# Loading down_w a second time and rounding it later, in a gated quantised MLP on one core

## The chip, the core and the metric

The kernel runs on one core of one Trainium2 chip. The metric is the device time in microseconds of one execution. A core has a matrix engine (PE, or TensorE), three engines for elementwise work (DVE or VectorE, ACT or ScalarE, POOL or GpSimd), a sequencer that issues nearly all DMAs of this kernel (SP or SyncE) and 16 DMA engines that carry them out. Each engine runs its own instructions in program order and waits on semaphores.

## The reference

x is 4 batches of 1024 tokens by 512. The weights are norm_w (512 by 128), up_w (4096 by 512) and down_w (512 by 2048).

```python
scale = cond @ norm_w.T + 1.0
ms = jnp.mean(x * x, axis=-1, keepdims=True)
h = x * (scale[:, None, :] * jax.lax.rsqrt(ms + EPS))
u = h @ up_w.T
val, gate = jnp.split(u, 2, axis=-1)
h = val * jax.nn.gelu(gate, approximate=False)
hq = act_quant(h)            # per token: round to -128..127 steps of max|h| / 127
wq = weight_quant(down_w)    # 1 / mean|down_w| as scale, round to -1, 0, 1
return hq @ wq.T + x
```

What matters here is weight_quant. It needs the mean of |down_w| over the whole matrix before the first element can be rounded, and its result, one of three values per element, is needed only by the second product.

## The kernel before

**Batches and slots.** The four batches are worked on one after the other, each in 16 slots (j is 0 to 15 within a batch, g is 16 b + j over all). One slot multiplies 128 rows of the gate half and 128 rows of the value half of up_w with the batch's 1024 tokens. Operands are split into a high and a low 16-bit part, so that a product is several matmuls added up in PSUM. The first batch uses the plain form: `plain_half(j, h)` is 12 matmuls of 512 columns for the gate (PSUM tile pg, line 601), a Gelu of it on ACT (line 629), 12 matmuls for the value (pv, line 601) and one DVE instruction that multiplies the two into H (line 633). h is 0 or 1, the half of the tokens. The later batches use a scheme with seven products of six matmuls in a slot (`slot`, products on line 586): PSUM tiles A, B and E, three ACT copies between them (lines 668, 675, 680) and two Gelus (lines 685, 701). In the first slot of the second batch (g = 16) two of the seven products belong to no slot before it and are missing.

**PSUM.** The tag "A" has two buffers, "B" one and "E" two. In the first batch pg of the first half lies in B, pg of the second half in A, and both pv in E. So the pv of one half waits until the DVE instruction of line 633 two halves earlier has read its bank, and line 633 waits for the Gelu of line 629.

**While the first batch runs**, the other engines prepare what the later batches need: they scale and split the rows of up_w and spill them to DRAM (s_dram; lines 355 and 400 on SP), and they normalise and split the tokens of the second batch in four groups of 256 (class `Tokens`, keys 6, 8, 10 and 12 in `TOKENS`: a group is normalised and summed in slot j and split by `high` and `low` and turned by a transposing DMA, `turn`, line 572, in slot j + 1). The tiles of a group are tagged xn (or am), xt and nx; each tag has one buffer. `turn` writes them into R[:, 1].

**down_w.** Eight parts of 128 by 1024 floats (512 KB each) are loaded into R[:, 1] at the start (`d_load`, line 444) and summed by absolute value (`d_sum`) up to slot 3; the mean is known in slot 4. `d_round(n)` multiplies part n by the scale and adds a large constant on ACT (line 464), `d_put(n)` takes the sign of the rounded part on ACT (line 473) and writes fp8 into a tile tn, two parts to one tile. After every second part a transposing DMA writes tn into wd (line 475). R[:, 1] is also where the turned tokens of the second batch go, so that the parts must be rounded before `turn` overwrites them: `D_ROUND` gives the slots. wd is read for the first time by the sums of weights in slots 9 and 10 of the second batch (`D_SUM_AT`).

**Fillers.** From the second batch on, two lists (`Filler`) hold DVE and ACT work; `run("x")`, `run("y")` and `run("z")` in a slot take items from their front as long as a budget lasts (on ACT 2.7 us at x and 1.1 us at y of an ordinary slot).

**SP order.** SP issues in program order, and it waits on behalf of a DMA before it issues it; what comes behind has to wait too. In slots 13 and 15 of the first batch, and in every slot of the second, it issues the loads of the weights for a slot that lies two ahead: `s_load_x(g)` brings the parts 5 and 6 (line 418, plain) and 0 to 2 (line 416, transposed), `s_load_y(g)` the rest. They go into SXY[:, (g + 1) % 2] and wait until the slot that used that buffer has been multiplied. The first product of a slot reads part 5, the second part 0, the fourth in time of g = 16 part 6.

A tile is handed on only when the last reader of its former content is done, also where that reader comes later in the program than the instruction that takes the buffer over.

Of the kernel before, what the change touches and what calls it, by code (L numbers as in the profile page):

```python
# [9 lines left out]
F32 = mybir.dt.float32  # L10
F16 = mybir.dt.float16
BF16 = mybir.dt.bfloat16
F8 = mybir.dt.float8e4
I32 = mybir.dt.int32
AF = mybir.ActivationFunctionType
# [4 lines left out]
P = 128  # L20
EXPONENT = 0x7F800000
MAGIC = 1.5 * 2.0**23
# [29 lines left out]
def glu_quant_kernel(  # L52
# [10 lines left out]
    PE, ACT, DVE, POOL, SP = nc.tensor, nc.scalar, nc.vector, nc.gpsimd, nc.sync  # L63
# [14 lines left out]
    wpool = ctx.enter_context(tc.tile_pool(name="work", bufs=2))  # L78
# [9 lines left out]
    unmagic = cpool.tile([P, 1], F32, name="unmagic")  # L88
# [24 lines left out]
    for n in range(0, P, 32):  # L113
        c = slice(n, n + 32)
# [118 lines left out]
    def cond_spread(dg, b0, b1, tag):  # L233
        n = b1 - b0
        pd = bank(tag, {"po": 3}.get(tag, 2), [P, B], f"pd_{b0}")[:, :n]
        PE.matmul(pd, ones[:n, :], dg, start=True, stop=True)
        return pd
# [42 lines left out]
    def w_load(j, ts=(1, 0)):  # L280
        if j > 2:
            SP.dma_start(out=wn(j), in_=up_v[j])
            return
        for t in ts:
            SP.dma_start(out=wn(j)[:, t], in_=up_v[j][:, t])
# [27 lines left out]
    def w_range(j, t0=0, t1=2):  # L313
        w_factor(j, w_largest(j, t0, t1), t0, t1)

    def w_gain(j):
        DVE.tensor_tensor(sg0[:, j, :], sw[:, j, :], dx[:, 0:1].to_broadcast([P, 2]), ALU.mult)
# [6 lines left out]
    def w_scale(j, ts=(1, 0), eng=None):  # L324
        eng = eng or (ACT if j >= ROWS else POOL)
        for t in ts:
            w, r = wn(j)[:, t], iv[j][:, t : t + 1]
            if eng is ACT:
                ACT.activation(w, w, AF.Copy, scale=r)
            else:  # L330
                eng.tensor_scalar(w, w, r, 1.0, ALU.mult, ALU.mult)
# [16 lines left out]
    def w_rows(j):  # L348

        v = H[:, ROW_SLOT.get(j, 15 + j % 2)].bitcast(F16).rearrange("p t d -> p (t d)")  # L350
        n = v.rearrange("p (n w f) -> p n w f", n=4, w=2)
        f = wn(j).rearrange("p t (n f) -> p (t n) f", n=2)
        ACT.copy(n[:, :, 0], f)
        DVE.tensor_tensor(n[:, :, 1], f, n[:, :, 0], ALU.subtract)
        SP.dma_start_transpose(
            s_tile(j)[:, 3:7].rearrange("p n w (k f) -> p (n w k) f", k=2), v
        )
# [19 lines left out]
    def s_sums(j):  # L377
        v = wn(j).rearrange("p t (n f) -> p t n f", n=2)
        a11, a12, a21, a22 = v[:, 1, 0], v[:, 1, 1], v[:, 0, 0], v[:, 0, 1]
        POOL.tensor_tensor(sf[:, 0], a21, a22, ALU.add)  # L380
        POOL.tensor_tensor(sf[:, 2], a11, a21, ALU.subtract)
        POOL.tensor_tensor(sf[:, 1], sf[:, 0], a11, ALU.subtract)
        POOL.tensor_tensor(sf[:, 3], a12, sf[:, 1], ALU.subtract)
# [6 lines left out]
    def s_high(j):  # L390
        for s, f in s_parts(j):
            ACT.copy(s[:, :, 0], f)
# [37 lines left out]
    wsc = cpool.tile([P, 1], F32, name="wsc")  # L430
    wsum = cpool.tile([P, 2 * NK], F32, name="wsum")
    HF = FF // 2
    ND = 2 * NK

    def d_part(n):
        return R[:, 1, n * HF : (n + 1) * HF]

    def d_at(n):

        return n // 4 + 2 * (n % 2), n // 2 % 2, n % 2  # L440
# [5 lines left out]
    def d_sum(n):  # L446
        jk = wpool.tile([P, HF], BF16, name=f"djk_{n}", tag="gm", bufs=1)
        ACT.activation(jk, d_part(n), AF.Abs, accum_out=wsum[:, n : n + 1])

    def d_total():  # L450
        part = sm.tile([P, 1], F32, name="wpart", bufs=1)
        DVE.tensor_reduce(part, wsum, AX.X, ALU.add)
        return part

    def d_mean(part):
# [2 lines left out]
        DVE.tensor_scalar(wmean, pm, 1.0 / (D * FF), 1e-5, ALU.mult, ALU.max)  # L458
        DVE.reciprocal(wsc, wmean)

    def d_round(n):

        dn = d_part(n)
        ACT.activation(dn, dn, AF.Copy, scale=wsc, bias=MAGIC)

    tn = []

    def d_put(n):
        _, u, y = d_at(n)
        if y == 0:  # L470
            tn.append(wpool.tile([P, HF], BF16, name=f"tn_{n}", tag="v"))
        t8 = tn[-1].bitcast(F8).rearrange("p (f y) -> p f y", y=2)
        ACT.activation(t8[:, :, y], d_part(n), AF.Sign, bias=unmagic, saturate=False)
        if y:
            SP.dma_start_transpose(wd[:, n // 4, u], tn[-1])

# [131 lines left out]
    def gains(b):  # L608
        sg[b] = sm.tile([P, NJ, 2], F32, name=f"sg_{b}", tag="sg")
        DVE.tensor_scalar(sg[b], sw, dx[:, b : b + 1], None, ALU.mult)  # L610
# [12 lines left out]
    def plain_half(j, h, between=nothing):  # L623
        whole = j == WHOLE
        tag = ("po", 3) if whole else ("A", 2) if h or j == 1 else ("B", 1)
        pg = bank(*tag, name=f"pg_{j}_{h}")
        plain(j, 1, h, pg)
        t1 = wpool.tile([P, TOK], F32, name=f"g_{j}_{h}", tag="t1")
        ACT.activation(t1, pg, AF.Gelu, scale=gain(j, 1))
        between()  # L630
        pv = bank(*(("po", 3) if whole and not h else ("E", 2)), name=f"pv_{j}_{h}")
        plain(j, 0, h, pv)
        DVE.scalar_tensor_tensor(h_half(j, h), pv, gain(j, 0), t1, ALU.mult, ALU.mult)
# [80 lines left out]
    def pair_max(b, i, h):  # L714

        v = h_slots(b * NJ + 2 * i, 2)[:, :, h].rearrange("p j t -> p t j")
        m = m_view(b, h)
        if i == 0:
            return [lambda: DVE.tensor_reduce(m, v, AX.X, ALU.max, apply_absolute_value=True)]
        gm = []  # L720

        def largest():
            gm.append(wpool.tile([P, TOK], F32, name=f"gm_{b}_{i}_{h}", tag="gm", bufs=1))
            DVE.tensor_reduce(gm[0], v, AX.X, ALU.max, apply_absolute_value=True)  # L724

        return [largest, lambda: DVE.tensor_tensor(m, m, gm[0], ALU.max)]  # L726
# [343 lines left out]


    D_SUM = {0: (4, 5), 1: (6, 7), 2: (2, 3), 3: (0, 1)}
    D_ROUND = {5: (0, 1), 6: (2,), 7: (3,), 9: (4,), 10: (5,), 11: (6,), 12: (7,)}
    D_MEAN = 4
    TOKENS = {6: 0, 8: 1, 10: 2, 12: 3}
    LARGEST = {
# [5 lines left out]
    def next_tokens(j):  # L1082

        if j in TOKENS:
            toks[j] = toks[j + 1] = Tokens(1, TOKENS[j])
            toks[j].load()

    def s_all(j):
        s_high(j)
        s_low(j, POOL)  # L1090
        s_spill(j)

    def first_batch(j, sc):

        if j + 2 <= LATE:
            w_load(j + 4)
        if j >= 4:
            next_tokens(j + 2)
        t = toks.get(j)
        odd = t is not None and j not in TOKENS  # L1100
        n = j + 2
        rows = LATE <= n < NJ
        if j + 1 < LATE:
            s_sums(j + 1)
        elif rows:
            s_sums(n)
        if j + 3 < NJ:
            w_range(j + 3)
            w_gain(j + 3)
        if j == D_MEAN:  # L1110
            part = d_total()
        plain_half(j, 0)
        for i, h in LARGEST.get(j, ()):
            for f in pair_max(0, i, h):
                f()
        if n < LATE:
            w_scale(n)
            w_rows(n)
        if j + 1 < LATE:
            s_all(j + 1)  # L1120
        if t and not odd:
            t.norm()
        for m in D_ROUND.get(j, ()):
            d_round(m)
            d_put(m)
        if t and not odd:
            t.scale(sc)
            t.sums()
        if j + 2 > LATE and j + 5 < NJ:
            w_load(j + 5)  # L1130
        if odd:
            t.high()
            t.low(DVE)
        if odd:
            t.turn()
        plain_half(j, 1)
        if j == 3:
            pd = cond_spread(dg, 1, B, "po")
            cond_undo(pd, 1, B)
            cond_rows()  # L1140
        if j == D_MEAN:
            d_mean(part)
        own = rows and j + 1 >= LATE

        def next_rows():
            if LATE <= j + 3 < NJ:
                w_scale(j + 3)
                w_rows(j + 3)

        if odd:  # L1150
            next_rows()
        if own:
            s_high(n)
            s_low(n, POOL)
        if not odd:
            next_rows()
        if own:
            s_spill(n)
        elif rows:
            s_sums(n)  # L1160
            s_all(n)
            w_load(j + 5)
        for n in D_SUM.get(j, ()):
            d_sum(n)
        if j in (NJ - 3, NJ - 1):
            s_load_x(NJ + (j - NJ + 3) // 2)
            s_load_y(NJ + (j - NJ + 3) // 2)
# [165 lines left out]
    state = {}  # L1333
    for b in range(1, B):
        dve, act = Filler(), Filler()
        gains(b)
        am = am_tile(b - 1)
        dq = state[b - 1] = sm.tile([P, 2 * NA], F32, name=f"dq_{b}", tag="dq")
# [120 lines left out]
    b = B - 1  # L1459
# [109 lines left out]
    for h in range(2):  # L1569
# [21 lines left out]
        for a in range(NA):  # L1591
            c, xr = slice(0, HALF * ys[a]), XR[:, h * NA + a]
            down_mm(b, h, a, pos[a][:, c], range(cut, NJ), 0, ys[a])
            down_end(b, h, a, pos[a][:, c], xr[:, c], dq, c)
    c = slice(HALF, D)
# [29 lines left out]
```

## Time and profile before

| what | value |
|---|---|
| median of 3 runs | 725.08 us (724.9 to 725.55) |
| profiled execution, first to last instruction | 724.0 us |
| PE busy | 716.5 us, 99% |
| DVE, ACT, POOL busy | 584.2, 397.6, 201.6 us |
| slots 13, 14, 15 of the first batch begin (PE) | 153.08, 163.44, 173.80 us |
| the second batch begins (PE) | 184.16 us |

The profiled execution's own time is the span of its instructions; the time of a run is taken around the whole program and includes what lies before the first and after the last instruction, here 1.1 us between the span and the median. In the profile's groups "idle before" is the time that an engine stood still just ahead of these instructions. PE's busy time is no measure of its peak, because matmuls overlap; the order of its matmuls in time, and what each waits for, says more.

### The profile page before, as it was taken

What the parts mean: (1) busy time and instruction counts of PE and PEld (TensorE: products, weight loads), DVE (VectorE), ACT (ScalarE), POOL (GpSimd) and SP (SyncE); (2) the same over time, 40 slices, a digit from 0 to 9 for tenths busy, and PEclk for the clock granted to TensorE, in tenths of its full rate; (3) what the DMA queues carried; (4) which work ended last, traced back from release to release, by engine and by line L of the source; (5) the groups of instructions that cost most, each with busy time, mean ns of one, the idle gap of its engine ahead of it and who ended that gap; (6) DMA issues with size and microseconds to landing.
All of it is one profiled execution on the core that took longest, in us unless ns stands there. A gap on an engine that the chain in (4) does not pass through costs nothing.

```text
span 724.0 us, 10200 instructions
## 1 busy us (share of the span) xinstructions
PE 716.5 (99%) x3678; PEld 359.9 (50%) x3678; DVE 584.2 (81%) x824; ACT 397.6 (55%) x625; POOL 201.6 (28%) x207
## 2 busy tenths in 40 slices
PE   7999999999999999999999999999999999999998
PEld 3544444444444446655444445666444444445854
DVE  8977999984698899887689897687678888755896
ACT  6768868861337674554335676544433665333473
POOL 1579788882100034440000030360020000000120
PEclk9999999999999999999999999999999999999999
DMA  9579999996654564977846646766955455453253
GB/s 317 190 231 271 300 287 251 276 229 152 117 103 102 132 150 127 208 174 167 174 102 103 131 102 176 200 155 159 216 105 103 101 104 100 102 101 97 103 174 119
DMA packets 224191, 117.85 MB, mean 163 GB/s; under 512 B 186486, under 2 KB 196871, under 8 KB 224140
## 3 DMA queue, kind: packets, MB, share of 16 engines
q1 hardware_dynamic: 223850, 116.87, 66.1%
q8 instruction: 29, 0.48, 0.3%
q10 hardware_dynamic: 290, 0.33, 0.1%
q14 instruction: 22, 0.18, 0.1%
HBM read 49.50 MB, written 23.09 MB: 100 GB/s over the span
## 4 chain that ended last, share of the span: by engine, by line
PE 98%; DMA 1%; ACT 0%; SPq 0%; issue 0%; DVE 0%; ACTq 0%
PE A L586 34%; PE E L586 17%; PE pg L601 11%; PE pv L601 11%; PE po L880 9%; PE B L586 9%; PE po_end L832 4%; DMA H<-in_x_dram 1%; PE ptx L981 1%; PE pv L648 0%; PE po_B L880 0%; PE pg L648 0%; PE pw L339 0%; PE po_A L880 0%; PE po_E L880 0%; ACT R L947 0%
## 5 line engine op out<-in xcount | busy, mean ns | idle before, releaser
L586 PEld LDWEIGHTS <-SXY 128*128 128x128 f16 x2016 | 196.9, 98 | 231.3 <-issue 0.6
L586 PE MATMUL A<-R,SXY 128*128 128x512 f16 x1152 | 266.0, 379 | 0.0
L586 PE MATMUL E<-R,SXY 128*128 128x512 f16 x576 | 140.0, 379 | 0.1
L688 DVE SCALAR_TENSOR_TENSOR H<-A,sg,t 128x512 f32<-128x512 f32 x48 | 36.0, 750 | 67.9 <-PE A L586 67.7
L740 POOL PARTITION_ALL_REDUCE am<-R x8 | 14.3, 1793 | 234.0 <-DVE R L726 234.0
L804 DVE TENSOR_TENSOR H<-H,am 128x1024 f32<-128x1024 f32 x64 | 76.1, 1215 | 0.0
L601 PEld LDWEIGHTS <-SXY 128*128 128x128 f16 x486 | 47.4, 98 | 57.4 <-DVE SXY L372 0.5
L701 ACT ACTIVATE t<-t,sg 128x512 f32<-128x512 f32 x48 | 34.6, 721 | 67.8 <-DVE t L698 67.7
L586 PE MATMUL B<-R,SXY 128*128 128x512 f16 x288 | 70.0, 379 | 0.0
L724 DVE TENSOR_REDUCE gm<-H 128x512 f32<-128x1024 f32 x56 | 69.0, 1233 | 1.0
L601 PE MATMUL pg<-R,SXY 128*128 128x512 f16 x252 | 58.0, 379 | 0.0
L601 PE MATMUL pv<-R,SXY 128*128 128x512 f16 x234 | 54.4, 380 | 0.0
L685 ACT ACTIVATE t<-B,sg 128x512 f32<-128x512 f32 x48 | 33.0, 687 | 36.3 <-PE B L586 36.3
L880 PE MATMUL po<-wd,R 128*128 128x256 fp8e4 x416 | 52.5, 273 | 0.0
L490 POOL TENSOR_SCALAR ssq<-ssq 128x2 f32<-128x2 f32 x12 | 4.3, 354 | 171.2 <-ACT xt L520 122.1
L668 ACT COPY t<-A 128x512 f32<-128x512 f32 x48 | 27.9, 582 | 39.8 <-PE A L586 39.5
L880 PEld LDWEIGHTS <-R 128*128 128x128 bf16 (+1 forms) x448 | 43.8, 98 | 9.0
L680 ACT COPY v<-E 128x512 f32<-128x512 f32 x48 | 28.1, 585 | 30.9 <-PE E L586 27.7
L675 ACT COPY B<-A 128x512 f32<-128x512 f32 x48 | 27.4, 572 | 30.5 <-PE A L586 30.0
L707 DVE SCALAR_TENSOR_TENSOR H<-v,sg,t 128x512 f32<-128x512 f32 x48 | 38.5, 802 | 6.6 <-ACT t L701 6.6
L812 ACT ACTIVATE H<-H 128x1024 f32<-128x1024 f32 x38 | 39.9, 1050 | 7.1 <-DVE H L804 7.1
L726 DVE TENSOR_TENSOR R<-R,gm 128x512 f32<-128x512 f32 x56 | 42.2, 753 | 1.3
(205 smaller groups left out, 986.8 us busy)
## 6 DMA issues: line engine op xcount, KB each, us to landing
SXY<-s_dram SPq DMA_DIRECT2D x48, 256.0 KB, 3.0
s_dram<-SXY SPq DMA_DIRECT2D x18, 384.0 KB, 3.3
H<-in_L_cond_up_w_dram SPq DMA_DIRECT2D x13, 512.0 KB, 5.7
SXY<-s_dram SPq DMA_DIRECT2D x48, 128.0 KB, 3.2
xr<-in_x_dram SPq DMA_DIRECT2D x19, 256.0 KB, 3.0
out_dram<-xr SPq DMA_DIRECT2D x19, 256.0 KB, 2.6
H<-in_x_dram SPq DMA_DIRECT2D x8, 512.0 KB, 6.7
R<-in_L_cond_down_w_dram SPq DMA_DIRECT2D x8, 512.0 KB, 7.4
```

The lines of the kernel that those rows point to most:

```text
L586: PE.matmul(o, s[:, w, k, :], tv[:, :, c, l, k, :], start=start and n == 0, stop=stop and n == len(TERMS) - 1, skip_group_check=True,)
L601: PE.matmul(ps, a[k // 2][:, w, k % 2, :], XP[:, l, k, h * TOK : (h + 1) * TOK], start=n == 0, stop=n == len(terms) - 1,)
L685: ACT.activation(cur["t1"], pb, AF.Gelu, scale=gain(g, 1))
L688: DVE.scalar_tensor_tensor(h_half(g - 1, 0), prev["A"], gain(g - 1, 0), prev["t1"], ALU.mult, ALU.mult)
L701: ACT.activation(prev["t2"], prev["t2"], AF.Gelu, scale=gain(g - 1, 1))
L707: DVE.scalar_tensor_tensor(h_half(g - 1, 1), prev["v"], gain(g - 1, 0), prev["t2"], ALU.mult, ALU.mult)
L724: DVE.tensor_reduce(gm[0], v, AX.X, ALU.max, apply_absolute_value=True)
L726: return [largest, lambda: DVE.tensor_tensor(m, m, gm[0], ALU.max)]
L804: DVE.tensor_tensor(v, v, r.to_broadcast([P, 2, TOK]), ALU.mult)
L812: ACT.activation(v, v, AF.Copy, bias=MAGIC)
L832: PE.matmul(po.rearrange("p (y c o) -> p y c o", c=2, o=P), q[:, a, h, j], wd8[:, :, j // n, j % n, :, y0:y1].rearrange("p c o y -> p y c o"),
L880: PE.matmul(po, w[:, j], m, start=start and j == 0, stop=stop and j == n - 1, skip_group_check=True,)
```

## The change

The rounding no longer reads the parts in R[:, 1]. Each part is loaded from DRAM a second time (`d_fetch`) into the buffer of xn, xt or nx, in turn, and rounded there: part 0 in slot 13 of the first batch, parts 1 and 2 in slot 14, 3 and 4 in slot 15, part 5 in slot 0 of the second batch, 6 and 7 in slots 1 and 2, the last three as items at the front of ACT's filler list. The first three loads are issued at the ends of slots 11, 12 and 13, load n + 3 right behind `d_put(n)`. The tile tn takes the buffers tagged xr, not v.

```diff
+    dn = {}
+
+    def d_fetch(n):
+
+        dn[n] = wpool.tile([P, HF], F32, name=f"dn_{n}", tag=("xn", "xt", "nx")[n % 3], bufs=1)
+        c, u, _ = d_at(n)
+        SP.dma_start(out=dn[n], in_=down_w[c * P : (c + 1) * P, u * HF : (u + 1) * HF])
+
     def d_round(n):
 
-        dn = d_part(n)
-        ACT.activation(dn, dn, AF.Copy, scale=wsc, bias=MAGIC)
+        ACT.activation(dn[n], dn[n], AF.Copy, scale=wsc, bias=MAGIC)
 
     tn = []
 
     def d_put(n):
         _, u, y = d_at(n)
         if y == 0:
-            tn.append(wpool.tile([P, HF], BF16, name=f"tn_{n}", tag="v"))
+            tn.append(wpool.tile([P, HF], BF16, name=f"tn_{n}", tag="xr"))
         t8 = tn[-1].bitcast(F8).rearrange("p (f y) -> p f y", y=2)
-        ACT.activation(t8[:, :, y], d_part(n), AF.Sign, bias=unmagic, saturate=False)
+        ACT.activation(t8[:, :, y], dn[n], AF.Sign, bias=unmagic, saturate=False)
+        if n + 3 < ND:
+            d_fetch(n + 3)
         if y:
             SP.dma_start_transpose(wd[:, n // 4, u], tn[-1])
...
-    D_ROUND = {5: (0, 1), 6: (2,), 7: (3,), 9: (4,), 10: (5,), 11: (6,), 12: (7,)}
+    D_FETCH = {11: 0, 12: 1, 13: 2}
+    D_ROUND = {13: (0,), 14: (1, 2), 15: (3, 4)}
+    D_LATE = ((5, 0), (6, 1), (7, 1))
...
         for n in D_SUM.get(j, ()):
             d_sum(n)
+        if j in D_FETCH:
+            d_fetch(D_FETCH[j])
         if j in (NJ - 3, NJ - 1):
             s_load_x(NJ + (j - NJ + 3) // 2)
             s_load_y(NJ + (j - NJ + 3) // 2)
...
     for b in range(1, B):
         dve, act = Filler(), Filler()
+        if b == 1:
+            for n, m in D_LATE:
+                act.add((m, "x"), 1.1, lambda now, n=n: d_round(n))
+                act.add((m, "x"), 1.1, lambda now, n=n: d_put(n))
```

## The prediction

> **What bounds the kernel now.** I read the page first, then the waits of PE, the chain in order of time around the end of the first batch, and last the timelines of ACT, DVE and SP there.
>
> ```profile
> span 724.0 us, 10200 instructions
> PE 716.5 (99%) x3678; PEld 359.9 (50%) x3678; DVE 584.2 (81%) x824; ACT 397.6 (55%) x625; POOL 201.6 (28%) x207
> PE 98%; DMA 1%; ACT 0%; SPq 0%; issue 0%; DVE 0%; ACTq 0%
> ...
> 70.00:150.00 80.00, 80.00 (x374) 36.31 (x373) 75.29 (x99) 63.22 (x94) 68.00 (x71) 1.00 1.07 272
> ```
>
> PE carries 98% of the chain. The last row is a stretch of 80 us that holds all eight roundings of today (columns: length; busy us and count of PE, weight loads, DVE, ACT, POOL; granted clock; DMA share; GB/s): PE is busy for 80.00 of 80.00 us at clock 1.00. So rounding costs PE nothing where it stands, and taking it away there can give PE nothing. What PE lacks over the whole span is 724.0 - 716.5 = 7.5 us. The change is therefore judged by one question: does the new place make PE wait? The chain there:
>
> ```profile
> 181.57 2.59 PE pv L601 x12
> 184.16 1.29 PE A L586 x6
> ...
> 188.04 1.29 PE B L586 x6
> 189.34 2.59 PE A L586 x12
> 191.93 1.29 PE E L586 x6
> 193.22 1.29 PE B L586 x6
> ...
> 198.41 2.59 PE A L586 x12
> 201.00 1.29 PE E L586 x6
> ```
>
> These (start, length) are my due times. 181.57 is the last pv of the first batch; 184.16 is g = 16; at 189.34 come six matmuls of g = 16 and then the first product of g = 17, at 190.63; 198.41 does the same for g = 17 and 18, so g = 18 begins at 199.70. Nothing is slack on PE, so a wait adds to the time one for one.
>
> **What is removed.** Eight ACT pairs and four transposing DMAs leave slots 5 to 12.
>
> ```profile
> L473 ACT ACTIVATE tn<-R,unmagic 128x1024 fp8e4<-128x1024 f32 x8 | 9.2, 1152 | 0.3
> L464 ACT ACTIVATE R<-R,wsc 128x1024 f32<-128x1024 f32 x8 | 9.1, 1136 | 0.0
> 152.41 1.64 SPq L475 DMA_TRANSPOSE wd<-tn x1
> ```
>
> One part is 1.14 + 1.15 = 2.29 us of ACT, eight parts 18.3 us. All of it lay beside a full PE: gain 0. Its bounds are 0 as well: a gain would have to come out of a PE wait in that stretch, and 80.00 of 80.00 leaves none; a loss can't come from work that is gone.
>
> **What is added, ACT.** The same 18.3 us come back in slots 13 to 18.
>
> ```profile
> 155.71 0.69 ACT L629 ACTIVATE g<-pg,sg 128x512 f32<-128x512 f32 x1 [1.16 <-PE pg L601]
> 156.29 0.91 ACT L565 CAST nx<-xa 128x512 f16<-128x512 f32 x2
> 157.97 1.04 ACT L565 CAST nx<-xt 128x1024 f16<-128x1024 f32 x1 [0.77 <-POOL xt L544]
> 171.25 0.69 ACT L629 ACTIVATE g<-pg,sg 128x512 f32<-128x512 f32 x1 [4.49 <-PE pg L601]
> 189.43 0.69 ACT L685 ACTIVATE t<-B,sg 128x512 f32<-128x512 f32 x1 [0.76 <-PE B L586]
> 192.02 0.57 ACT L675 COPY B<-A 128x512 f32<-128x512 f32 x1 [1.91 <-PE A L586]
> 194.62 0.69 ACT L685 ACTIVATE t<-B,sg 128x512 f32<-128x512 f32 x1 [0.77 <-PE B L586]
> 197.15 0.59 ACT L668 COPY t<-A 128x512 f32<-128x512 f32 x1 [1.84 <-PE A L586]
> ```
>
> In slots 14 and 15 ACT stands idle 4.49 us ahead of a Gelu, and two parts are 4.58 us: as pure work they fit, 0.1 us over. In g = 16 the pair follows the Gelu that ends at 190.12 and ends at 192.41; the copy into B then runs to 192.98 and is due at 193.22. In g = 17 the pair ends at 195.31 + 2.29 = 197.60, the copy at 198.19, due at 198.41. Both fit with 0.2 us to spare; I take 0, bounds 0 and 0.3 each. What hides them is thin, so each tenth that ACT runs late there costs a tenth.
>
> **What is added, loads and waits.** Eight loads of 512 KB. Where the trace has one of this size:
>
> ```profile
> H<-in_L_cond_up_w_dram SPq DMA_DIRECT2D x1, 512.0 KB, 3.8
> H<-in_L_cond_up_w_dram SPq DMA_DIRECT2D x1, 512.0 KB, 5.1
> H<-in_L_cond_up_w_dram SPq DMA_DIRECT2D x1, 512.0 KB, 6.8
> ```
>
> These are three loads of the same kind and size, all from the stretch of the first row above; they differ in what stands ahead of them in the DMA engines. I take 3.8 where the queue is short, 5.1 where it is full, 6.8 as the far bound. The order on SP and the work it meets:
>
> ```profile
> 158.37 0.75 DVE L633 SCALAR_TENSOR_TENSOR H<-pv,sg,g 128x512 f32<-128x512 f32 x1 [2.50 <-PE pv L601]
> 159.03 1.87 DVE L569 TENSOR_TENSOR nx<-xa,nx 128x512 f16<-128x512 f32 x2
> 160.82 1.75 DVE L569 TENSOR_TENSOR nx<-xt,nx 128x1024 f16<-128x1024 f32 x1
> 162.60 4.31 SPq L572 DMA_TRANSPOSE R<-nx x1
> SXY<-H SPq DMA_TRANSPOSE x1, 4.3
> 155.93 1.86 SPq L355 DMA_TRANSPOSE SXY<-H x1
> 181.60 0.33 SPq L418 DMA_DIRECT2D SXY<-s_dram x1
> 181.98 2.69 SPq L416 DMA_TRANSPOSE SXY<-s_dram x1
> SXY<-s_dram SPq DMA_TRANSPOSE x1, 6.1
> SXY<-s_dram SPq DMA_TRANSPOSE x1, 4.5
> SPq L418 <- PE pg L601: 8.8, 2, 8.7
> ```
>
> Step 1, load 0 takes the place on SP of the removed transpose at 152.41 and lands at 156.2 (3.8) to 157.5 (5.1). ACT is free from 156.4, so part 0 is rounded by 158.7 to 159.8, ahead of the split of the last token group, whose `low` on DVE ended at 160.82 + 1.75 = 162.57. DVE had begun it at 159.03; now its first half can start 0.4 to 1.6 us later. End of `low`: 163.0 to 164.2.
>
> Step 2, load 1 takes xt, which `low` reads last. It stands on SP ahead of load 3 and of `turn` (162.60). Behind it SP holds nothing that PE needs before g = 16. With two issues of about 0.4 us (by the 0.33 of the 181.60 row), `turn` goes out at 163.8 to 165.0 and takes 4.31 us to issue.
>
> Step 3, load 2 takes nx, which `turn` reads, so it waits until `turn` has landed. The smaller transpose at 155.93 landed 4.3 us after its start, 2.4 us behind its issue's end. By that `turn` lands at 163.8 + 4.3 + 2.4 = 170.5 at best. Loads 1 and 3 stand ahead of it: the 6.8 row against the 3.8 row says that a loaded queue costs up to 3.0 us, which I halve for the late end: 165.0 + 6.7 + 1.5 = 173.2. Load 2 lands at L2 = 174.3 (170.5 + 3.8) to 178.3 (173.2 + 5.1); middle 176.3. All this time ACT stands in slot 14 before part 2, and behind it is the second Gelu of slot 14, which ran at 171.25.
>
> Step 4, what L2 may be. (a) Rounding 2.29, Gelu 0.69 and line 633 at 0.75 free the E bank for the pv at 181.57: L2 at most 177.8. (b) Part 2, two Gelus, parts 3 and 4 (three pairs 6.87, two Gelus 1.38), a third Gelu 0.69 and the copy 0.57 are 9.5 us and due at 188.04: L2 at most 178.5. (c) `s_load_x(17)` stands behind load 7, which waits for part 4: L2 + 8.3 + 0.4. Its first part, at 3.8, is due at 190.63: at most 178.1. Its transposed parts go out 0.4 us later and land after 4.5 to 6.1 us, due at 191.93: L2 at most 176.7 to 178.3. So the point from which PE waits is 177.5, give or take 0.8, and the middle L2 is 1.2 us ahead of it. In this term I take a wait of 0 to 0.3 us, bounds 0 and 178.3 - 176.7 = 1.6 us. (The limits don't add: a wait at (a) shifts (b) and (c) with it.) `s_load_x(16)` leaves SP behind load 2, at about 173 by step 3; due at 184.16, it has 11 us.
>
> A rule that would change the sum: the Trainium skill, page "DMA: Bandwidth & Descriptors", section "Anatomy of one DMA", fits one transfer (from another issuing engine) as about 2.0 us plus its bytes at 436 GB/s, an estimate of 3.2 us for 512 KB. By it L2 would be 173.7 to 176.4 (170.5 and 173.2 plus 3.2), and no limit of step 4 would be reached; the rows have 3.8 at the least, so I keep them. The same section says that a wait is made by the issuing sequencer and not by the DMA engines, which speaks against this change: it is what puts `turn` behind load 1. The trace agrees: the last of the rows above is SP itself, waiting up to 8.7 us for a matmul ahead of a load of weights.
>
> **Sum.** Removed 0, ACT in g = 16 and 17 about 0.1, the chain through load 2 about 0.2: span 724.3, and with the 1.1 us around it 725.4 us.
>
> **Rivals.** (1) Slower: load 2 is late. The point is L2 = 177.5. If all loads meet a full queue (6.8 us), load 0 lands at 159.2, `low` ends at 165.9, `turn` goes out at 166.7 and lands at 173.4 to 176.4, and L2 is 180.2 to 183.2: PE waits 2.7 to 5.7 us at 181.57 or at g = 17, for 728 to 731. For it speaks that DMA is at share 1.07 up to 150 us and that the chain has five links, each of which I took near its good end; against it that the big transposes thin out after slot 12. For a PE wait of this length the Trainium skill, page "TensorE: Matmul & The Clock Gate", section "HAM oscillation", states that idling over about 3.4 us halves the clock for a while. That would put something on top only at the far end of this rival; the clock of 1.00 in the rows here can't show it.
>
> (2) Slower by less: the transposes of tn, now on SP in g = 16 and g = 18, hold up the loads behind them. The first waits for part 5 at 192.41, takes 1.64 us, and `s_load_x(18)` goes out at 194.0, lands by 4.5 to 6.1 at 198.9 to 200.5 for the transposed part that is due at 201.00, its plain part at 197.9 for 199.70. It fits by 0.5 us; late by the 3.0 us of a full queue it costs 2.5 us: 727.9. The point is 201.00. Against it speaks that only loads 6 and 7 are in the queue by then.
>
> (3) Faster: less ACT and SP work in slots 5 to 12 lets PE go on sooner. The 80.00 of 80.00 row excludes more than hundredths there, and the time would be that of before, 725.1.
>
> **How the numbers follow.** A measurement of this kernel can tell about 0.2% (1.45 us) from no change: below 723.6 is faster, above 726.5 slower. Forecast, a wait under 1.45 us: 0.57. Rival 1: 0.32. Rival 2: 0.08. So slower is 0.40. Rival 3 by more than 1.45 us: 0.03, for what no row shows. The range starts at 724.7, a little below the lowest of the three runs (724.9), and reaches to 729.5, the middle of rival 1, so that about 0.16 is left out above and 0.03 below. The forecast's own range is 724.8 to 726.5.
>
> **What would show it.** Right: the lines of `d_round` and `d_put` lie between 156 and 207 us; ACT stands 5 to 8 us in slot 14 before part 2, released by a DMA; the Gelu that ran at 171.25 runs near 179; `turn` starts 1 to 3 us after 162.60; SP waits for it before load 2; PE shows no wait over 0.5 us, and g = 16 begins within 0.5 us of 184.16. Wrong: a PE wait of over 1.5 us at pv of slot 15, at B of g = 16 or at A or E of g = 17 (rival 1), or at g = 18 (rival 2). The forecast fails if load 2 lands after 178.5, or if a tile's wait turns out to hold another place in SP's order than I read from the code.

## The result and the profile after

| | median | runs |
|---|---|---|
| before | 725.28 us | 724.9 to 726.1, 5 runs |
| changed | 728.73 us | 727.32 to 729.96, 5 runs |

The ratio is 1.0047, 95% interval 1.0033 to 1.006: slower by 3.45 us (by the medians), beyond the 0.2% that a measurement can tell. It lies inside the range given, at the near end of rival 1, while the forecast was no visible change. The profiled execution of the changed kernel has a span of 727.0 us, 3.0 more than before. In the changed kernel line 586 is 595, 601 is 610, 629 is 638, 633 is 642, 464 is 471, 473 is 480, 572 is 581, the copy into B, 675, is 684, and the second loads are line 467.

The page of the changed kernel: span, busy time, chain by engine.

```profile
span 727.0 us, 10207 instructions
PE 717.8 (99%) x3678; PEld 360.5 (50%) x3678; DVE 581.4 (80%) x824; ACT 397.9 (55%) x625; POOL 202.0 (28%) x207
PE 72%; DVE 9%; DMA 6%; POOL 6%; issue 4%; ACT 2%; SPq 1%; POOLq 0%; DVEq 0%; ACTq 0%
```

The shares of busy time have hardly moved, and ACT's sum is the same (397.9 against 397.6), yet the chain is no longer PE alone: followed back from the end, it leaves PE at 193.2 us, where PE waits for weights, and goes on through loads, ACT, DVE and POOL. What PE waited for, from 21 us on (before: nothing):

```profile
PE A L595 <- DMA SXY<-s_dram: 2.1, 1, 2.1
PE pv L610 <- DVE H L642: 0.8, 1, 0.8
```

Those two waits are 2.9 us together. Up to them this execution runs 0.5 us ahead of before (the Gelu of 155.71 is at 155.23); behind them it is 2.9 us late (a product that began at 194.36 begins at 197.24). So they moved PE by 3.4 us: PE's rows show six matmuls as 1.46 us although the next six begin after 1.29 (184.00 and 185.29 in the kernel before), so that each wait shows nearly 0.2 us too short. Their place, in the chain of the changed kernel (start, length):

```profile
172.03 6.04 DMA dn<-in_L_cond_down_w_dram
...
186.79 6.39 DMA SXY<-s_dram
193.18 0.05 issue
193.23 1.47 PE A L595 x6
```

The first is load 2, on which the pv of slot 15 waits through ACT and DVE; the second is the plain part of the weights for g = 17. ACT and DVE of the changed kernel there (the bracket is the idle time before an instruction and what ended it):

```profile
156.58 1.15 ACT L471 ACTIVATE dn<-dn,wsc 128x1024 f32<-128x1024 f32 x1 [0.66 <-DMA dn<-in_L_cond_down_w_dram]
178.09 1.15 ACT L471 ACTIVATE dn<-dn,wsc 128x1024 f32<-128x1024 f32 x1 [8.40 <-DMA dn<-in_L_cond_down_w_dram]
180.32 1.25 ACT L638 ACTIVATE g<-pg,sg 128x512 f32<-128x512 f32 x2
185.91 0.67 ACT L638 ACTIVATE g<-pg,sg 128x512 f32<-128x512 f32 x1
```

```profile
161.04 1.74 DVE L578 TENSOR_TENSOR nx<-xt,nx 128x1024 f16<-128x1024 f32 x1
181.08 1.41 DVE L642 SCALAR_TENSOR_TENSOR H<-pv,sg,g 128x512 f32<-128x512 f32 x2 [8.19 <-ACT g L638]
```

ACT stands 8.40 us in slot 14 before part 2. Behind it the Gelu that ran at 171.25 runs at 180.32, and DVE frees the E bank only after that. SP of the changed kernel:

```profile
162.81 0.81 SPq L467 DMA_DIRECT2D dn<-in_L_cond_down_w_dram  x2
163.68 6.25 SPq L581 DMA_TRANSPOSE R<-nx  x1
...
172.03 0.62 SPq L467 DMA_DIRECT2D dn<-in_L_cond_down_w_dram  x1
...
178.82 0.53 SPq L467 DMA_DIRECT2D dn<-in_L_cond_down_w_dram  x1
...
186.04 0.66 SPq L467 DMA_DIRECT2D dn<-in_L_cond_down_w_dram  x1
186.79 0.42 SPq L418 DMA_DIRECT2D SXY<-s_dram  x1
```

These are loads 1 and 3, the turn of tokens, load 2, load 4, load 7, and then the weights for g = 17, which left at 181.60 before.

### The profile page after: what moved, and what is told of

Same layout as the page of the kernel before. It is cut to its first block, busy times and chain, and to the rows that moved or that the text cites. A ratio compares the mean times of both kernels' runs of the same rounds, so it can differ in the third digit from the quotient of the medians.

```text
span 727.0 us, 10207 instructions
## 1 busy us (share of the span) xinstructions
PE 717.8 (99%) x3678; PEld 360.5 (50%) x3678; DVE 581.4 (80%) x824; ACT 397.9 (55%) x625; POOL 202.0 (28%) x207
## 4 chain that ended last, share of the span: by engine, by line
PE 72%; DVE 9%; DMA 6%; POOL 6%; issue 4%; ACT 2%; SPq 1%; POOLq 0%; DVEq 0%; ACTq 0%
PE A L595 32%; PE E L595 16%; PE po L889 9%; PE B L595 8%; PE po_end L841 4%; DMA dn<-in_L_cond_down_w_dram 2%; DVE gm L733 1%; DMA H<-in_L_cond_up_w_dram 1%; DMA R<-nx 1%; DVE wam L290 1%; POOL R L396 1%; POOL H L383 1%; DMA s_dram<-R 1%; DVE nx L578 1%; DMA SXY<-s_dram 1%
```

## The experiments

The order theory says that the loss is ACT standing before loads that land late, and the weights for g = 17 standing on SP behind load 7, which waits for ACT. The volume theory says that 4 MB more keep the DMA engines full, whatever the order. The ACT theory says that 18.3 us of rounding are too much work in slots 13 to 18. The code cuts are shortened; `...` stands for lines left out. In the kernels whose code has `issue`, lines 595 to 684 of the changed kernel are 600 to 689.

**The loads without the late rounding.**

```diff
 (the kernel before)
+    D_AGAIN = {13: (3,), 14: (4, 5), 15: (6, 7)}
...
         for m in D_ROUND.get(j, ()):      # still slots 5 to 12, from R
             d_round(m)
             d_put(m)
+        for m in D_AGAIN.get(j, ()):
+            d_fetch(m)
```

Loads 0 to 2 are added at the ends of slots 11 to 13 as in the change; nothing reads the eight loaded parts.

> The kernel before, with the eight second loads added at the same places of SP's order, but nothing reads them: the parts are rounded from R in slots 5 to 12 as before. Order theory: no ACT instruction stands between a load and the next, SP has issued all loads before the weights of g = 17 are due, PE waits under 0.3 us, 725.0 to 725.6. Volume theory: the same 4 MB are moved in the same stretch, so most of the loss stays, 727 to 729. ACT theory: 725.0 to 725.6, as by the order theory.

Measured: 725.81 us against 725.52, ratio 1.0003 (0.9994 to 1.0012). PE shows no wait after 21 us. The windows of before, then of this kernel (last two columns: DMA share and GB/s):

```profile
172.00:178.00 6.00, 6.00 (x30) 2.69 (x29) 2.08 (x3) 0.69 (x1) 0.38 (x1) 1.00 0.50 95
178.00:184.00 6.00, 6.00 (x30) 2.69 (x29) 4.51 (x5) 0.69 (x1) 0.00 (x0) 1.00 0.19 50
```

```profile
172.00:178.00 6.00, 6.00 (x30) 2.74 (x28) 2.03 (x3) 0.69 (x1) 0.38 (x1) 1.00 1.02 277
178.00:184.00 6.00, 6.00 (x30) 2.71 (x28) 4.51 (x5) 0.69 (x1) 0.00 (x0) 1.00 1.04 307
```

The DMA engines go from a share of 0.50 and 0.19 to full, and PE is busy for all of both windows. The bytes alone cost nothing; the volume theory falls. (Bytes in the queue can still make a later transfer land later; that costs time only where something waits for it.)

**Only the last three parts late.** Parts 0 to 4 are rounded from R in slots 5 to 9.

```diff
+        if n < 5:
+            dn[n] = d_part(n)
...
-        if n + 3 < ND:
-            d_fetch(n + 3)
...
+    D_FETCH = {11: 6, 12: 7, 13: 5}
+    D_ROUND = {5: (0, 1), 6: (2,), 7: (3,), 9: (4,)}
```

> Parts 0 to 4 are rounded from R in slots 5 to 9 as before; parts 5, 6 and 7 alone are loaded again (at the ends of slots 13, 11 and 12) and rounded in the second batch's slots 0 to 2. Order theory: nothing in slots 13 to 15 waits for ACT, and the three late pairs fit beside the copies: PE waits under 0.3 us, 725.0 to 725.8. If the tight fit in the second batch's first slots (0.2 us to spare) or the transposes ahead of the weights there were what costs: 726.5 to 728.

Measured: 724.99 us against 725.5, ratio 0.9998 (0.9989 to 1.0007), no PE wait after 21 us. The thin fit in g = 16 to 18 and the transposes beside the weights there (rival 2) cost nothing. The loss belongs to what this kernel leaves out: the late rounding of parts 0 to 4, and loads that wait behind it.

**SP's order alone.**

```diff
 d_put:
         if n + 3 < ND:
-            d_fetch(n + 3)
+            issue(n, lambda: d_fetch(n + 3))          # n = 3 and 4: kept back
         if y:
-            SP.dma_start_transpose(wd[:, n // 4, u], tn[-1])
+            issue(n, lambda t=tn[-1]: SP.dma_start_transpose(wd[:, n // 4, u], t))
 end of slot 15, behind s_load_x and s_load_y for g = 17:
+            for f in behind:
+                f()
```

`issue` runs at once what it is given, except for n = 3 and 4: those wait in the list `behind` until the weights have been issued.

> The changed kernel, but loads 6 and 7 and the transpose of parts 2 and 3 are issued behind the loads of the weights for g = 17, not ahead of them; ACT's order is unchanged. Order theory: the wait of 2.1 us at the first product of g = 17 goes, that of 0.8 us at the pv of slot 15 stays, 726.0 to 726.5. Volume theory: 728 to 729. ACT theory: 728 to 729, since ACT does the same work at the same places.

Measured: 726.15 us against 725.52, ratio 1.0012 (1.0004 to 1.0021), as the order theory had it. ACT's instructions and their order are those of the changed kernel, so the ACT theory falls here for most of the loss; 0.6 us stay. One line of SP and one of ACT in this kernel:

```profile
181.73 0.33 SPq L418 DMA_DIRECT2D SXY<-s_dram  x1
```

```profile
177.59 1.15 ACT L471 ACTIVATE dn<-dn,wsc 128x1024 f32<-128x1024 f32 x1 [8.03 <-DMA dn<-in_L_cond_down_w_dram]
```

The weights leave at 181.73, not 186.79, and the wait at g = 17 is gone. Part 2 starts at 177.59; in this execution, which runs 0.1 us behind before, the pv of slot 15 doesn't wait either. In the change, which runs 0.5 us ahead, 178.09 cost 0.8 us: the limit of 177.8 in step 4 (a) is about right. So this profile shows what takes the wait at g = 17 away, and not that the other stays; where the 0.6 us come from isn't shown.

**Part 2 in slot 15.**

```diff
-    D_ROUND = {13: (0,), 14: (1, 2), 15: (3, 4)}
+    D_ROUND = {13: (0,), 14: (1,), 15: (2, 3, 4)}
```

> The changed kernel with part 2 rounded in slot 15, not in slot 14; loads and their order on SP unchanged. Order theory: ACT reaches the second Gelu of slot 14 before it waits for load 2, so the wait at the pv of slot 15 goes; load 7 is issued about 1 us earlier, the weights for g = 17 still stand behind it and come about 2 us late: 726.8 to 727.8. If the wait of ACT in slot 14 were the whole cause, both waits would go: 725.0 to 725.8. ACT theory: three parts in slot 15 are more than its idle time, 729 or more.

Measured: 727.48 us against 725.5, ratio 1.0033 (1.0021 to 1.0045). The one wait of PE in the profile of this kernel:

```profile
PE A L595 <- DMA SXY<-s_dram: 1.1, 1, 1.1
```

The wait at the pv is gone, that for the weights of g = 17 is not, as expected. So the two waits can be taken away one without the other.

**Load 2 ahead of the turn.**

```diff
-tag=("xn", "xt", "nx")[n % 3]
+tag="am" if n == 2 else ("xn", "xt", "nx")[n % 3]
-    D_FETCH = {11: 0, 12: 1, 13: 2}
+    D_FETCH = {11: (0,), 12: (1, 2)}
```

> Part 2 is loaded into the buffer tagged am and issued right behind load 1, ahead of the last turn of tokens; all else as in the changed kernel. Order theory (load 2 comes late because SP issues it behind that turn and the spill, and the loads of the weights for g = 17 come late because they stand behind load 7): ACT no longer stands 8.4 us before part 2, the 0.8 us wait of PE at the pv of slot 15 goes; load 4 still stands behind the weights of g = 16, so the first product of g = 17 still waits 1 to 2 us; 726.3 to 727.5. Volume theory (4 MB more keep the DMA engines full, whatever the order): 728 to 729 as in the changed kernel. ACT theory (18.3 us of ACT work in slots 13 to 18 are too much there): 728 or more.

Measured: 730.7 us against 725.52, ratio 1.0073 (1.0061 to 1.0085): slower than the change. The order theory had 726.3 to 727.5 and the volume theory 728 to 729; only the "728 or more" of the ACT theory covers it, but not by its reason, for ACT waits here more than it works (0.72 us busy from 178 to 184). The wait of PE, the turn on SP, ACT in slot 15 and a window of this kernel:

```profile
PE A L595 <- ACT B L684: 3.7, 1, 3.7
```

```profile
164.70 8.36 SPq L581 DMA_TRANSPOSE R<-nx  x1
```

```profile
170.57 1.15 ACT L471 ACTIVATE dn<-dn,wsc 128x1024 f32<-128x1024 f32 x1 [0.42 <-DMA dn<-in_L_cond_down_w_dram]
...
185.08 1.15 ACT L471 ACTIVATE dn<-dn,wsc 128x1024 f32<-128x1024 f32 x1 [6.36 <-DMA dn<-in_L_cond_down_w_dram]
187.59 1.15 ACT L480 ACTIVATE tn<-dn,unmagic 128x1024 fp8e4<-128x1024 f32 x1 [1.37 <-DMA wd<-tn]
```

```profile
187.00:193.20 6.20, 3.35 (x9) 1.21 (x9) 2.73 (x4) 3.31 (x5) 0.91 (x1) 0.72 1.13 315
```

The first half came as expected: ACT waits 0.42 us before part 2, not 8.40. But three loads ahead of the turn lengthen its issue to 8.36 us, everything behind it on SP slides, load 4 among it, and ACT now stands 6.36 us in slot 15 before part 4 and 1.37 more for the buffer of the tile that part 4 is written to. The second Gelu of slot 15 and the copy into B stand behind that, and PE waits 3.7 us in g = 16. The wait was moved to a place with less room, not removed.

**Both, load 2 early and the late loads behind.** The edits of "SP's order alone" and "Load 2 ahead of the turn", together.

> Both edits in one kernel: load 2 early, and loads 6, 7 and the transpose of parts 2 and 3 behind the weights of g = 17. Order theory: both waits go, PE waits under 0.4 us, 725.0 to 725.8, the time of the kernel before although all the added loads and the late rounding are there. Volume theory: 728 or more. ACT theory: 728 or more.

Measured: 728.99 us (725.91 to 732.23, 10 runs) against 725.52, ratio 1.0051 (1.0031 to 1.0072); a miss, at a time that the volume and the ACT theory would have too. Three of the ten are under 727; the profiled one is the slowest. Its wait of PE, and ACT before part 4:

```profile
PE A L600 <- ACT B L689: 5.9, 1, 5.9
```

```profile
187.58 1.15 ACT L471 ACTIVATE dn<-dn,wsc 128x1024 f32<-128x1024 f32 x1 [9.21 <-DMA dn<-in_L_cond_down_w_dram]
```

The same place as in the kernel with load 2 early, for the same reason: load 4 comes too late, which moving loads 6 and 7 doesn't touch. In this execution load 0 was late as well (part 0 starts at 158.55, in the change at 156.58), so that not all of the 5.9 us is the edits'.

**Loads from ACT's queue.**

```diff
-        SP.dma_start(out=dn[n], in_=...)
+        (SP if n < 3 else ACT).dma_start(out=dn[n], in_=...)
 and the transpose of parts 2 and 3 behind the weights of g = 17
```

> The changed kernel, but loads 3 to 7 are issued by ACT right behind the Sign that frees their buffer, not by SP, and the transpose of parts 2 and 3 stands behind the weights of g = 17 on SP. Every load and every ACT pass stays. Order theory: SP's queue carries none of the loads that wait for ACT, load 4 is there early, the weights of g = 17 leave at 181 to 182: no wait at g = 17, 0 to 0.8 us at the pv of slot 15, 725.0 to 726.3. If the DMA engines' own queue were the cause and not SP's order: 727 to 729.

Measured: 729.22 us against 725.5, ratio 1.005 (1.0037 to 1.0063); a miss in time, above both ranges that were given. Its waits of PE, and ACT around one of its loads:

```profile
PE pv L615 <- DVE H L647: 2.2, 1, 2.2
PE A L600 <- ACT B L689: 1.0, 1, 1.0
```

```profile
179.22 1.15 ACT L471 ACTIVATE dn<-dn,wsc 128x1024 f32<-128x1024 f32 x1 [7.70 <-DMA dn<-in_L_cond_down_w_dram]
180.40 1.15 ACT L480 ACTIVATE tn<-dn,unmagic 128x1024 fp8e4<-128x1024 f32 x1
181.58 0.34 ACTq L467 DMA_DIRECT2D dn<-in_L_cond_down_w_dram  x1
182.02 1.27 ACT L643 ACTIVATE g<-pg,sg 128x512 f32<-128x512 f32 x2 [0.47 <-ACT tn L480]
```

One half came as expected: no wait at g = 17. But part 2 starts at 179.22, later still, and each load costs ACT 0.4 to 0.5 us between the Sign and the next instruction, just where ACT is late. Taking loads off SP didn't help here, where ACT waits for them. How much of it is the edit's stays open: load 0, which SP still issues, landed 2.2 us later than in the change (part 0 starts at 158.76), and that moved the whole chain; the fastest of the six runs had 727.48 us.

**Everything later.**

```diff
-    D_ROUND = {13: (0,), 14: (1, 2), 15: (3, 4)}
-    D_LATE = ((5, 0), (6, 1), (7, 1))
+    D_ROUND = {14: (0,), 15: (1,)}
+    D_LATE = ((2, 0), (3, 1), (4, 2), (5, 3), (6, 4), (7, 5))
```

> The changed kernel with every part rounded at least a slot after its load can have landed: part 0 in slot 14, part 1 in slot 15, parts 2 to 7 one to a slot in the second batch's slots 0 to 5; loads 0 to 2 at the same places, the others behind the Sign that frees their buffer, as in the change. Lead theory (the loss is ACT standing before loads 2 and 4 that land too late, and the weights of g = 17 queued behind loads that wait for ACT; neither the work nor the bytes cost anything): ACT waits for no load, PE waits under 0.4 us, 725.0 to 725.8. If ACT's work or the transposes beside the weights in the second batch cost something: 726.5 to 729.

Measured: 731.12 us against 725.39, ratio 1.0074 (1.0061 to 1.0087); a miss, above both ranges that were given. The wait of PE and ACT just before its end:

```profile
PE B L595 <- ACT B L684: 3.4, 1, 3.4
```

```profile
264.12 1.04 ACT L821 ACTIVATE H<-H 128x1024 f32<-128x1024 f32 x1
265.19 1.06 ACT L825 ACTIVATE R<-H 128x1024 bf16<-128x1024 f32 x1
...
268.80 0.58 ACT L684 COPY B<-A 128x512 f32<-128x512 f32 x1
```

There is no wait left in slots 13 to 18, as the theory says. But six pairs at the front of ACT's filler list take the room of the quantising passes (lines 821 and 825), which then come in a row when they are due: nine of them from 258.70 on, in slots 8 and 9 of the second batch, where the kernel before has five. They hold up the copy into B, which ran at 265.10 before. Rounding is work that ACT can take in slots 5 to 12, but not for nothing everywhere.

**Part 2 in slot 15 and loads 6 and 7 behind.** The edits of those two kernels together.

> Part 2 rounded in slot 15 (as in the kernel that moved it there) and loads 6 and 7 and the transpose of parts 2 and 3 behind the weights of g = 17. Lead theory: ACT reaches the second Gelu of slot 14 before it waits for load 2, and the weights of g = 17 no longer stand behind load 7: both waits go, 725.0 to 726.0. If one of them only moves to load 4, ahead of the second Gelu of slot 15: 726.5 to 728.

Measured: 726.28 us (724.78 to 732.09, 12 runs) against 725.39, ratio 1.002 (1.0001 to 1.004), between the two ranges that were given. Some executions take as long as before, some far longer; the profiled one took 731.64 us. Its wait of PE, and ACT at part 0:

```profile
PE A L600 <- ACT B L689: 3.5, 1, 3.5
```

```profile
161.06 1.15 ACT L471 ACTIVATE dn<-dn,wsc 128x1024 f32<-128x1024 f32 x1 [4.34 <-DMA dn<-in_L_cond_down_w_dram]
```

Part 0 started at 161.06, 4.5 us later than in the profile of the change, and the whole chain behind it slid: it's the place that the second range was given for, ACT ahead of the second Gelu of slot 15.

**Load 0 earlier.** Two kernels: the one above and the plain change, each with this edit.

```diff
         if odd:
             t.turn()
+        if j == 11:
+            d_fetch(0)
-    D_FETCH = {11: 0, 12: 1, 13: 2}
+    D_FETCH = {12: 1, 13: 2}
```

> As the kernel with part 2 in slot 15 and loads 6 and 7 behind the weights of g = 17, and load 0 is issued right behind the turn of tokens in slot 11, ahead of two transposes and spills, not at the slot's end. Lead theory: ACT never waits for load 0, so the late executions (up to 732) go with the waits: median 725.0 to 725.8 and no run over 727. If the late executions come from elsewhere, the median stays near 726.3 with runs up to 732.

> The changed kernel with load 0 alone issued earlier (right behind the turn of slot 11). Lead theory: the chain load 0, low, turn, load 2 moves forward by what ACT waited for load 0 (0.7 us in the profile of the changed kernel, more in late executions); the wait at the pv of slot 15 goes, most of that at the first product of g = 17 stays, since the weights still stand behind load 7: 726.5 to 728. If load 0 is not where the chain begins: 728.5 to 729, as in the changed kernel.

Measured: with both other edits 725.92 us (725.01 to 727.7, 11 runs) against 725.63, ratio 1.0001 (0.9992 to 1.001), a little over the 725.8 and the 727 that were given; the change with load 0 earlier alone 727.96 us (726.4 to 733.18, 11 runs), ratio 1.0047 (1.0027 to 1.0066). Part 0 on ACT in the first:

```profile
155.52 1.14 ACT L471 ACTIVATE dn<-dn,wsc 128x1024 f32<-128x1024 f32 x1
```

The wait of PE in the second:

```profile
PE A L595 <- DMA SXY<-s_dram: 2.2, 1, 2.2
```

In the first, ACT doesn't wait for load 0, PE waits nowhere after 21 us, and the time is that of before with all 4 MB, all late rounding and the same slots but one part. It doesn't beat before; none of these kernels does by more than the measurement can tell. In the second the pv's wait is gone and that for the weights stays, as expected; but it still has executions of 730 to 733, which load 0 therefore doesn't explain alone (for the clock in them see the last section).

## Why the prediction was right and where it was wrong

The time lies in the range, but not by the mechanism that was forecast; the range had room for a rival, and that the rival's own figure fits is in part luck.

**What bounds the kernel** held: PE had no wait to give back, so taking the rounding out of slots 5 to 12 gained nothing, and every wait added came out (2.9 us of waits, 3.0 us of span). That a wait costs just its length didn't hold everywhere: see the clock in the last section.

**Steps 1 and 2** held. Part 0 started at 156.58, `low` ended at 161.04 + 1.74 = 162.78 (given: 163.0 to 164.2), the turn went out at 163.68 (163.8 to 165.0). Since this execution runs 0.5 us ahead, both lie within what was given.

**Step 3** named the right chain and mis-sized a term. The issue of the turn was taken at its old 4.31 us and took 6.25, with loads 1 and 3 ahead of it; but the late end had allowed for a full queue, and the turn landed at 172.0, inside the 170.5 to 173.2 given. Load 2 was taken at 3.8 to 5.1 us and took 6.04, behind the turn and the spill. So part 2 started at 178.09, or 178.6 by the clock of before: just past the late end of 178.3, and not at the middle of 176.3.

**Step 4** set the right limits. With L2 = 178.6 limit (a), 177.8, was passed by 0.8 us, which is the wait at the pv. In (c), the term that failed most, the weights of g = 17 left when step 4 says (L2 + 8.3 + 0.4, that is 186.8), but their plain part was taken to land after 3.8 us and took 6.39; loads 6 and 7 and a transpose had been issued within 3 us ahead of it. That wait was 2.1 us. The kernel with SP's order changed shows that it hangs on that order.

**The forecast** of 0 to 0.3 us for this term was thus wrong. ACT stood in slot 14 before part 2 as foretold (8.40 us against 5 to 8). Of rival 1, a late load 2, the places came true: pv of slot 15 and A of g = 17. Its links did not: it has load 0 land at 159.2, `low` end at 165.9 and load 2 land at 180.2 to 183.2, and these were 156.6, 162.8 and 178.1. By its own rule, L2 less 177.5, the wait would have been 1.1 us. That the 2.9 us measured lie near its low end of 2.7 is luck: most of them come from the weights' 6.39 us, which rival 1 didn't price. The error was to take links of one chain one by one near their good ends.

**Rivals 2 and 3**: no wait at g = 18, and the kernel with the last three parts alone late is as fast as before. No gain was found.

**Around the span** I took 1.1 us, from one execution's profile and the median of three runs. Wherever a run's own span is on record, before or changed, the difference is 1.7 to 1.9 us (728.73 against 727.0 here). That moves the forecast's total by 0.7 us, not the comparison.

**Open**: why some executions issue load 0 or the later links several us late. The kernel before has no wait that hangs on them, the changed one has.

## What to carry to other kernels

When every added load fits by itself, add up the chain in which one load waits for what an earlier one held up, and take all links at the loaded duration, not the best one. An engine that waits for a load holds up all that stands behind it in program order: put such a step where its data has long landed, and issue what another engine needs soon ahead of what waits. Moving one load forward (here load 2 ahead of the turn) can make things worse, because it lengthens whatever now stands behind it on the same queue.

## What the runs showed of the hardware

The issue of a DMA grew with what stood ahead of it: the last turn of tokens held SP for 4.31 us with no load directly ahead, 5.3 to 5.6 with one load of 512 KB (three kernels), 6.1 to 6.7 with two and 8.2 to 8.4 with three. The share of the first load isn't certain, since the earlier turns, with no load ahead, took 4.2 to 5.4 us.

A wait of PE can cost more than its length. In the kernel with load 2 early, PE waited 3.7 us and the granted clock was then 0.72 over the 6.2 us of the window quoted there; PE's waits were 3.7 us and its median 5.2 us above before. In these runs the length of the wait alone doesn't decide it. The wait of 2.1 us in the changed kernel left the clock at 1.00, and so did the one of 3.4 us in the profile of the kernel with everything later (four other executions of it have a mean clock of 0.995 to 0.998); but behind the wait of 2.2 us in the change with load 0 earlier, at the same product as in the change, the clock fell to half (the third number from the right):

```profile
194.00:196.00 2.00, 2.00 (x6) 0.69 (x5) 0.00 (x0) 0.57 (x1) 1.06 (x1) 0.50 0.88 207
```

The span of that execution is 4.0 us above before, with 2.2 us of waits. Of the eleven executions of that kernel the five over 729 us have a mean clock of 0.998, the six under 728 us have 1.0. The Trainium skill, page "TensorE: Matmul & The Clock Gate", section "HAM oscillation", puts the limit at about 3.4 us of idling. These runs don't agree with it as a limit: 2.2 us was enough in one, 3.4 us was not in another. What else decides it stays open. Of the five runs of the change, the clock doesn't explain the spread: one of 729.95 us had a mean clock of 1.0, one of 729.96 us had 0.998.
